# A graph layer and an attention layer on one core: late x one slot ahead, and a new order of vector work from the sixth values to the end of the projections

## The chip, the cores and the metric

The kernel runs on one core of one Trainium2 chip. The metric is the device time of one execution, in microseconds. A core has five engines that take their instructions in program order and wait for each other through semaphores: PE (TensorE, matrix products), DVE (VectorE), ACT (ScalarE), POOL (GpSimd) and SP (SyncE, which here only issues DMA transfers; ACT issues some too).

## The reference, cut to what matters

x has 64 batches of 256 nodes with 512 channels; adj is a 256 x 256 matrix of zeros and ones.

```python
# layer 0: graph
a = adj.astype(x.dtype); deg = a.sum(axis=1)
mi = einsum('bkd,od->bko', x, Wi);  mj = einsum('bkd,od->bko', x, Wj)
x = layernorm(x + deg[None, :, None] * (mi + b) + einsum('ij,bjo->bio', a, mj))
# layer 1: attention, 8 heads of 64 channels
q, k, v = (split_heads(x @ W.T + bias) for W, bias in (...))
attn = softmax(where(adj == 0, -inf, q @ k.T / 8))
x = layernorm(x + (attn @ v) @ Wo.T + bo)
```

All of it is float32.

## The kernel before

The 64 batches go in 32 groups of two. A batch is two tiles t = 1, 0 of 128 nodes. The steps of neighbouring groups are interleaved by hand: turn g of the loop at L1132 (31 turns) finishes the attention of group g, runs layer 0 for the batches b1 = 2(g+1) and b2 = b1 + 1 of the next group, and ends with the next group's projections to q, k and v and its first two scores. b3 = b1 + 2 is a batch whose x is fetched ahead.

Float32 products are split. A factor is cut into a head (rounded on ACT, `split_head`, L680), a diff (DVE, `split_diff`, L683: head times a constant minus the source) and a low part (source minus head, `split_low`, L686, on DVE or POOL as its argument says). A product is then three matrix products, into two PSUM banks: heads and lows into X, diffs into Y. ACT takes X out of its bank, DVE adds Y. The weights are kept in DRAM in this cut form and come through a ring of seven buffers (`factor`); `bring` (L445) fetches the next one when one has been used. In the loop its orders stand on SP, or on ACT in the middle of the output projection.

The attention of a group is eight pairs of heads w = 0 to 7, the first four for the first batch. For each, `scores` (L896) puts its products on PE at once and returns the rest as a function (`now()`, `later()`): DVE adds the mask (L910), ACT takes the exponential (L914), POOL adds two halves for the denominators (`pk`, L924). `values` (L935) is the product with v. `divide_two` (L954) runs after every second pair: ACT copies the values to aoT (L958), PE sums the denominators (`den`), DVE takes the reciprocal into `spread` (L1009), two DMAs copy halves of spread to the other partitions (L1012). `multiply` (L949) multiplies aoT by spread on POOL (L952). With `apart=True` the step from the reciprocal on is returned as `invert`; in the last one the sum of inverses is returned as `total_up`.

aoT is then cut for the output projection: `ao_parts(g, i, cs)` is batch i of the group, with the channel chunks `upper` (0, 1; pairs 0 and 1 of the batch) or `lower` (2, 3). The buffers of q, k and v are free by then and take the three parts, so that in the profile qT, kT and v hold head, diff and low part. `o_steps` (L821) is that projection: `begin` and `go_on` for the first batch's tile 0, `own` for its tile 1, `others` for the second batch's tiles, with `adds` for their sums on DVE (L830, L833). PE runs straight from `others` into the first values projection, `v[0]`, whose bank must have been freed by `adds(1)`.

Layer 0 of b1 and b2 are the objects `first` and `second`. `add` adds the neighbours' sum to x (DVE, L613), `stat` takes the statistics of layernorm (four DVE instructions, L496 to L502, and a power on POOL, L504), `give` applies them (two ACT instructions, L509, L510). The result h has to be turned for the projections: `send_h` writes a tile to DRAM (SP, L702), `fetch_h` reads it back in another order (SP, L707), `turn_h` turns it on DVE into hF (L517); then it is cut into hA, hD, hL. Within `others` the same is done for b2.

x comes twice: `load_x` (L294) for the sums, 512 KB into one of five buffers xh (the late x), and `load_xB` (L302), four DMAs, for the transposed form, which `turn_x` turns on DVE and `x_head`, `x_diff`, `x_low` cut on ACT, DVE and POOL. `finish_steps` (L875) gives six steps for the group that is done: `end[0]`, `end[2]` statistics, `end[1]`, `end[3]` their application, `end[4]`, `end[5]` the stores. `add_bias` and `add_output_bias` are two additions on POOL (L368, L733).

Every engine's order is that of the Python program: each instruction passes through

```python
    def in_order(ins):
        tc.keep_in_program_order(ins)
```

so the order of the calls in the loop is the order on each engine's queue, and two calls that use different engines can change places without changing either queue.

Of the kernel before, what the change touches and what calls it, by code (L numbers as in the profile page):

```python
# [219 lines left out]
def unshifted_path(ctx, tc, flag, x, adj, wiT, wjT, b0, wqT, bq, wkT, bk, wvT, bv, woT, bo, out):  # L220
# [16 lines left out]
    nc = tc.nc  # L237
# [56 lines left out]
    def load_x(b):  # L294
        if b < B:
            xh[b] = p5.tile([P, NT, D], F32, tag="xh", name="xh")
            in_order(nc.sync.dma_start(out=xh[b], in_=x[b].rearrange("(t p) d -> p t d", p=P)))
# [147 lines left out]
    def bring(several=1, left=1, issuer=None):  # L445
        for _ in range(several):
            if queue:
                name, j, first = queue.pop(0)
                f = stream.tile([P, 3, D], F32R, tag="factor", name="factor")
                coming.append(f)  # L450
                if first:
                    begin_make(f, name, j)
                    end_makes(left)
                else:
                    end_makes()
                    in_order((issuer or nc.sync).dma_start(out=f.bitcast(F32), in_=kept[name][j]))
# [216 lines left out]
    def three(tags):  # L673
        return [p1.tile([P, NC, NB * N], F32R, tag=t, name=t) for t in tags]
# [4 lines left out]
    def split_head(parts, src):  # L679
        in_order(nc.scalar.activation(parts[0], src, AF.Identity, scale=DOWN))  # L680
# [4 lines left out]
    def split_low(parts, src, engine):  # L685
        in_order(engine.tensor_tensor(parts[1], src, parts[0].bitcast(F32), ALU.subtract))  # L686
# [18 lines left out]
    def fetch_h(b, t):  # L705
        hB[b, t] = p1.tile([P, P // R, P], F32, tag=f"hB{t}", name="hB")
        in_order(nc.sync.dma_start(out=hB[b, t].rearrange("p a n -> p (a n)"),  # L707
                                   in_=h_cols[b][t].rearrange("q (r a) n -> (q r) (a n)", r=R)))
# [226 lines left out]
    def values(g, w):  # L935
        i, pr = divmod(w, NC)
        if w == 0:
            aoT[g] = p1.tile([P, NC, NB * N], F32, tag="aoT", name="aoT")
        pp = w % 2
        if pp == 0:  # L940
            pavs[g] = value_bank("pav").rearrange("p (r q) -> p r q", r=2)
        pe, _ = made[g, w]
        for kc in range(NT):
            for q in range(P // R):
                d0 = 2 * pr * DH + channels(q).start
                matmul(pavs[g][q * R:(q + 1) * R, pp ^ (q // 2), :], vv[g][:, i, kc, d0:d0 + R], pe[:, q % 2, kc, :],
                       start=(kc == 0), stop=(kc == NT - 1), tile_position=(0, q * R))

    def multiply():  # L949
        while products:  # L950
            d, spread = products.pop()
            in_order(nc.gpsimd.tensor_tensor(d, d, spread, ALU.mult))  # L952
# [34 lines left out]
    def ao_parts(g, i, cs):  # L987

        cols = slice(i * N, (i + 1) * N)
        return cut_parts(aoP[g], cs, cols), aoT[g][:, cs, cols]  # L990
# [32 lines left out]
    def run(steps):  # L1023
        for s in steps:
            s()
# [77 lines left out]
    v, q_, k = projection_steps(0, "SMSM", False)  # L1103
# [28 lines left out]
    for g in range(NG - 1):  # L1132
        b1, b2, b3 = NB * (g + 1), NB * (g + 1) + 1, NB * (g + 2)
        every, upper, lower = slice(0, NC), slice(0, 2), slice(2, NC)
        if g == 0:
            fold_value_bias()
            add_bias(b2)
            first.graph_half(1)
            first.take(1)
            first.cut_up(1)  # L1140
            make_first("wi", 0)
            first.graph_half(0)
            first.take(0)
            first.cut_up(0)
            make_first("wi", 1)
            first.own_half(0)
            end_makes()
        else:
            first.streamed = second.streamed = coming[1:1 + NC]
            k[NC - 1]()  # L1150
            x_head(b2)
            x_low(b2)
            add_bias(b2)
            first.graph_half(0, (0, 2, 1))
            first.take(0)
            x_diff(b2)
            first.own_half(1, kind="S")
            first.own_half(0, kind="S")
            first.cut_up(0)

        values(g, 0)
        values(g, 1)
        divide_two(g, 1)
        run([scores(g, 2), scores(g, 3)])
        load_xB(b3)
        second.own_half(1)
        if g == 0:
            make_first("wi", 2)
        second.own_half(0)
        if g:  # L1170
            for _ in range(NC):
                coming.pop(0)
                bring()

        values(g, 2)
        values(g, 3)
        multiply()
        if g == 0:
            make_first("wi", 3)
            end_makes()  # L1180
        early = cut_early(g)
        split_head(*early)
        divide_two(g, 3)
        now, later = scores(g, 4), scores(g, 5)
        now()
        second.graph_half(1, (0, 2, 1))
        second.take_x(1)
        later()
        second.take_y(1)
        split_diff(*early)  # L1190
        split_low(*early, nc.gpsimd)
        first.neighbours()
        second.graph_half(0, (0, 2, 1))
        second.cut_up(1)
        first.add(1)
        first.add(0)
        second.take(0)
        first.stat(1)
        second.cut_up(0)
        first.give(1)  # L1200
        send_h(b1, 1)

        values(g, 4)
        values(g, 5)
        load_x(b3)
        multiply()
        if g == 0:
            add_output_bias(0)
            add_output_bias(1)
        first.stat(0)  # L1210
        invert = divide_two(g, 5, True)
        now, later = scores(g, 6), scores(g, 7)
        aoP[g] = three(("qT", "kT"))
        aoP[g].insert(1, None)
        now()
        split_head(*ao_parts(g, 0, lower))
        begin, go_on, own, adds, others = o_steps(g, early[0], lambda t: turn_h(b2, t))
        begin()
        later()
        second.neighbours()  # L1220
        values(g, 6)
        invert()
        fetch_h(b1, 1)
        values(g, 7)
        split_diff(*ao_parts(g, 0, lower))
        second.add(0)
        aoP[g][1], = three(("v",))
        first.give(0)
        multiply()
        second.add(1)  # L1230
        send_h(b1, 0)
        total_up = divide_two(g, 7)
        split_head(*ao_parts(g, 1, upper))
        fetch_h(b1, 0)
        go_on()
        split_low(*ao_parts(g, 0, lower), nc.gpsimd)
        own()
        h11 = turn_h(b1, 1)
        split_head(*h11)
        second.stat(1)  # L1240
        second.give(1)
        split_low(*ao_parts(g, 1, upper), nc.vector)
        split_diff(*ao_parts(g, 1, upper))
        multiply()
        split_head(*ao_parts(g, 1, lower))
        second.stat(0)
        adds(0)
        split_low(*ao_parts(g, 1, lower), nc.gpsimd)
        second.give(0)
        split_diff(*ao_parts(g, 1, lower))  # L1250
        h10 = turn_h(b1, 0)
        send_h(b2, 1)
        send_h(b2, 0)
        split_diff(*h11)
        split_head(*h10)
        adds(1)
        split_low(*h10, nc.vector)
        split_diff(*h10)
        total_up()
        fetch_h(b2, 1)  # L1260
        fetch_h(b2, 0)
        split_low(*h11, nc.gpsimd)
        first, second = Layer0(b3) if b3 < B else None, Layer0(b3 + 1)
        v, q_, k = projection_steps(g + 1)
        end = finish_steps(g)
        others()
        turn_x(b3)
        if g == 0:
            make_first("wj", 0)
            make_first("wj", 1)  # L1270
        v[0]()
        if g == 0:
            make_first("wj", 2)
            make_first("wj", 3)
            end_makes()
        x_head(b3)
        x_low(b3)
        v[1]()
        x_diff(b3)
        load_xB(b3 + 1)  # L1280
        run([end[0], q_[0], end[1], k[0], end[2], q_[1]])
        if first:
            first.graph_half(1, (0, 2, 1))
            first.take(1)
        run([end[3], k[1], end[4]])
        add_output_bias(b1)
        if g + 2 < NG:
            add_bias(b3)
        run([q_[2]])
        load_x(b3 + 1)  # L1290
        add_output_bias(b2)
        if first:
            first.cut_up(1)
        run([k[2], q_[3], end[5]])
        turn_x(b3 + 1)
        run([scores(g + 1, 0), scores(g + 1, 1)])
        if g + 2 == NG:
            k[3]()
# [93 lines left out]
```

## Time and profile before

| what | value |
|---|---|
| median of 3 runs | 2952.39 us (2951.73 to 2953.07) |
| profiled execution: device time | 2951.97 us |
| profiled execution: span | 2950.1 us |
| PE busy | 2878.1 us (98%) |
| DVE, POOL, ACT busy | 2265.1, 1482.3, 1309.4 us |
| granted PE clock | 0.999 |
| one turn of the loop (from 1403.11 to 1493.52) | 90.41 us; PE 88.97, DVE 70.71, POOL 46.01, ACT 40.30 busy |
| HBM traffic | 227 GB/s over the span, 239 GB/s in that turn |

The profile is of one execution. A row of a timeline gives the start, the duration (of so many merged instructions, x1, x4), the engine, the source line, the operation, and out<-in by the program's names with shapes. A bracket at the end gives the time that the engine sat idle before it, and what ended that. Instructions of DVE, ACT and POOL overlap by about 0.1 us where one follows another at once. The ends of matmuls are modelled: the busy time of PE includes some slack that only shows in the distance between starts. PE's rows all have line L286, the helper through which it is issued.

### The profile page before, as it was taken

Reading aid. Unit: us, or ns where it says so; the run is one execution under the profiler, and the core shown is the slowest. Engines: PE = TensorE matmul, PEld = TensorE weight load, DVE = VectorE, ACT = ScalarE, POOL = GpSimd, SP = SyncE. Lnnn points to the kernel's source line nnn. Section 1 sums busy time; section 2 is a strip of 40 time slices with the busy share of each in tenths; the row PEclk is TensorE's granted clock in tenths of the full one; section 3 lists DMA queues with packets and bytes.
Section 4 is the critical chain, followed back from the end, with each engine's and each line's share of the span. In section 5 each row is a group of like instructions: output and inputs, shape, how many; then the busy total and the mean of one; then the engine's idle time right before and its main releaser. Section 6 shows DMA issues by size and latency. Waiting matters only on the chain.

```text
span 2950.1 us, 45509 instructions
## 1 busy us (share of the span) xinstructions
PE 2878.1 (98%) x16902; PEld 2140.1 (73%) x16902; DVE 2265.1 (77%) x3275; ACT 1309.4 (44%) x2412; POOL 1482.3 (50%) x1049
## 2 busy tenths in 40 slices
PE   9999999999999999999999999999999999999998
PEld 6577777777777777777777777777777777777775
DVE  5777787777877778877778777787777787777875
ACT  4444444444444444444444444444444444444443
POOL 3555555454555455454545544555545555454553
PEclk9999999999999999999999999999999999999999
DMA  7577766777666776667776677766677766777653
GB/s 251 194 258 239 247 218 218 255 245 266 217 219 239 266 247 230 212 226 264 242 247 222 221 249 252 268 212 215 238 267 240 246 214 215 257 248 261 213 211 116
DMA packets 303345, 690.54 MB, mean 234 GB/s; under 512 B 25744, under 2 KB 171280, under 8 KB 302864
## 3 DMA queue, kind: packets, MB, share of 16 engines
q1 hardware_dynamic: 282784, 588.02, 58.4%
q10 hardware_dynamic: 20336, 99.56, 9.5%
q8 instruction: 136, 2.23, 0.3%
q14 instruction: 89, 0.73, 0.1%
HBM read 589.04 MB, written 81.79 MB: 227 GB/s over the span
## 4 chain that ended last, share of the span: by engine, by line
PE 77%; DVE 15%; POOL 3%; DMA 3%; issue 1%; SPq 1%; ACT 1%; POOLq 0%; DVEq 0%; ACTq 0%
PE px L286 26%; PE pxy L286 20%; PE py L286 13%; PE ps L286 7%; PE pav L286 5%; PE pa L286 3%; DVE hF L517 2%; DMA hB<-h_cols 2%; DVE kT L683 2%; DVE spread L1009 2%; DVE st L496 2%; PE po L286 2%; DVE xh L833 1%; PE den L286 1%; DVE xh L830 1%
## 5 line engine op out<-in xcount | busy, mean ns | idle before, releaser
L924 POOL TENSOR_TENSOR pk<-pe 128x512 f32<-128x512 f32 x256 | 347.4, 1368 | 729.5 <-ACT pe L914 729.5
L914 ACT ACTIVATE pe<-pe 128x1024 f32<-128x1024 f32 x256 | 271.0, 1059 | 176.9 <-DVE pe L910 176.9
L504 POOL TENSOR_TENSOR rstd<-ve,mhalf 128x1 f32<-128x1 f32 x256 | 167.5, 654 | 343.4 <-DVE below L502 313.2
L910 DVE TENSOR_TENSOR pe<-ps,maskT 128x1024 f32<-128x1024 f32 x256 | 297.2, 1200 | 3.6 <-PE ps L286 3.6
L1009 DVE RECIPROCAL spread<-den 128x256 f32<-128x256 f32 x127 | 222.7, 1754 | 81.7 <-ACT aoT L958 51.8
L686 POOL TENSOR_TENSOR hL<-hF,hA 128x512 fp32r<-128x512 f32 x93 | 166.4, 1789 | 229.1 <-ACT hA L680 229.1
L774 DVE TENSOR_TENSOR kT<-py,kT 128x512 f32<-128x512 f32 x128 | 88.5, 692 | 226.2 <-ACT kT L773 226.2
L286 PE MATMUL ps<-qT,kT 64*128 64x256 f32 x2048 | 256.6, 390 | 0.0
L286 PE MATMUL pav<-pe,v_sb 128*32 128x256 f32 x4096 | 248.4, 382 | 3.5 <-DVE kT L774 1.5
L286 PEld LDWEIGHTS ps<-qT,kT 64*128 64x128 f32 x2048 | 187.3, 187 | 68.6 <-PE pav L286 26.3
L510 ACT ACTIVATE xh<-xh,shift,rstd 128x512 f32<-128x512 f32 x256 | 208.8, 816 | 8.6
L286 PEld LDWEIGHTS pav<-pe,v_sb 128*32 128x32 f32 x4096 | 120.0, 110 | 116.8 <-issue 24.4
L680 ACT ACTIVATE hA<-hF 128x512 fp32r<-128x512 f32 x124 | 78.3, 632 | 278.5 <-DVE hF L517 255.5
L286 PE MATMUL px<-factor,x_head 128*128 128x512 f32 x720 | 200.2, 400 | 0.0
L286 PE MATMUL py<-factor,x_diff 128*128 128x512 f32 x720 | 192.8, 390 | 2.0 <-ACT kT L773 2.0
L368 POOL TENSOR_TENSOR xh<-xh,degb 128x1024 f32<-128x1024 f32 x64 | 182.5, 2853 | 22.8 <-ACT degb L365 20.9
L286 PE MATMUL px<-factor,x_low 128*128 128x512 f32 x720 | 192.8, 390 | 0.0
L952 POOL TENSOR_TENSOR aoT<-aoT,spread 128x512 f32<-128x512 f32 x127 | 165.9, 1306 | 41.6 <-DMA spread<-spread 35.4
L686 POOL TENSOR_TENSOR x_low<-xT,x_head 128x1024 fp32r<-128x1024 f32 x60 | 144.2, 2403 | 67.6 <-ACT x_head L680 64.7
L286 PE MATMUL py<-hD,factor 128*128 128x512 f32 x640 | 175.9, 397 | 2.2 <-ACT kT L773 2.2
L286 PE MATMUL px<-hA,factor 128*128 128x512 f32 x640 | 175.7, 397 | 0.0
L496 DVE BATCH_NORM_STATS2 st<-xh 128x6 f32<-128x512 f32 x256 | 174.3, 681 | 0.2
(160 smaller groups left out, 6809.1 us busy)
## 6 DMA issues: line engine op xcount, KB each, us to landing
factor<-wi SPq DMA_DIRECT2D x120, 768.0 KB, 8.7
factor<-wo SPq DMA_DIRECT2D x120, 768.0 KB, 6.2
factor<-wv SPq DMA_DIRECT2D x93, 768.0 KB, 7.8
factor<-wk SPq DMA_DIRECT2D x93, 768.0 KB, 7.0
factor<-wq ACTq DMA_DIRECT2D x62, 768.0 KB, 7.6
factor<-wq SPq DMA_DIRECT2D x62, 768.0 KB, 7.4
xB<-in_x_dram SPq DMA_DIRECT2D x256, 128.0 KB, 4.1
xh<-in_x_dram SPq DMA_DIRECT2D x64, 512.0 KB, 3.9
```

What stands on the lines that cost most here:

```text
L286: in_order(nc.tensor.matmul(*args, **kw))
L368: in_order(nc.gpsimd.tensor_tensor(xh[b], xh[b], degb, ALU.add))
L496: order(nc.vector.bn_stats(st, t))
L504: order(nc.gpsimd.tensor_tensor(rstd, ve, mhalf, ALU.pow))
L510: order(nc.scalar.activation(t, t, AF.Identity, bias=shift, scale=rstd))
L686: in_order(engine.tensor_tensor(parts[1], src, parts[0].bitcast(F32), ALU.subtract))
L774: in_order(nc.vector.tensor_add(dst, Y, dst))
L910: in_order(nc.vector.tensor_add(pe.rearrange("p j t q -> p j (t q)"), ps.rearrange("p j t q -> p j (t q)"), maskT.rearrange("p t q -> p (t ...
L914: in_order(nc.scalar.activation(flat, flat, AF.Exp, scale=QSCALE, accum_out=etot[:, NB * g + i, pr:pr + 1]))
L924: in_order(nc.gpsimd.tensor_tensor(pk, pe[:, :, 0, :], pe[:, :, 1, :], ALU.add))
L952: in_order(nc.gpsimd.tensor_tensor(d, d, spread, ALU.mult))
L1009: in_order(nc.vector.reciprocal(rden, den))
```

## The change

`load_x(b3)` moves from after the sixth values (`values(g, 5)`) to before the third (`values(g, 2)`); it is behind the factors that `bring` fetches there. From the seventh scores to the end of the projections the calls are put in a new order. No call is added or left out. One changes its engine: the low part of b1's tile 0 (`split_low(*h10, ...)`) goes from DVE to POOL. The order on PE is the same as before.

On DVE: both `second.add` stand ahead of the first `split_diff`; `second.stat(0)` ahead of the upper `split_diff`; `x_diff(b3)` ahead of the sums of `v[1]`; `end[2]` after the sums of `q_[1]`; the `lo` of `first.cut_up(1)` after the sums of `k[2]`. On ACT: the split of the lower half of the first batch is ahead of the exponentials of `scores(g, 6)`; `end[3]` is after `k[1]`; `hi` of `cut_up` after `k[2]`. On POOL: `split_low(*h10)` after `split_low(*h11)`, and `add_bias(b3)` ahead of `add_output_bias(b1)`. On SP: `load_x(b3)` as said; the four DMAs of `load_xB(b3 + 1)` ahead of the four factors that `v[1]` brings; one factor ahead of `load_x(b3 + 1)`.

```diff
@@ 
                 bring()
+        load_x(b3)
 
         values(g, 2)
@@ 
         values(g, 5)
-        load_x(b3)
         multiply()
@@ 
+        split_head(*ao_parts(g, 0, lower))
         now()
-        split_head(*ao_parts(g, 0, lower))
         begin, go_on, own, adds, others = o_steps(g, early[0], lambda t: turn_h(b2, t))
         begin()
         later()
         second.neighbours()
         values(g, 6)
         invert()
+        second.add(1)
+        first.give(0)
+        values(g, 7)
+        aoP[g][1], = three(("v",))
         fetch_h(b1, 1)
-        values(g, 7)
+        second.add(0)
+        send_h(b1, 0)
+        multiply()
         split_diff(*ao_parts(g, 0, lower))
-        second.add(0)
-        aoP[g][1], = three(("v",))
-        first.give(0)
-        multiply()
-        second.add(1)
-        send_h(b1, 0)
         total_up = divide_two(g, 7)
-        split_head(*ao_parts(g, 1, upper))
-        fetch_h(b1, 0)
         go_on()
         split_low(*ao_parts(g, 0, lower), nc.gpsimd)
         own()
         h11 = turn_h(b1, 1)
+        second.stat(1)
+        split_head(*ao_parts(g, 1, upper))
         split_head(*h11)
-        second.stat(1)
         second.give(1)
+        multiply()
         split_low(*ao_parts(g, 1, upper), nc.vector)
-        split_diff(*ao_parts(g, 1, upper))
-        multiply()
+        fetch_h(b1, 0)
         split_head(*ao_parts(g, 1, lower))
         second.stat(0)
+        split_diff(*ao_parts(g, 1, upper))
+        split_low(*ao_parts(g, 1, lower), nc.gpsimd)
         adds(0)
-        split_low(*ao_parts(g, 1, lower), nc.gpsimd)
         second.give(0)
         split_diff(*ao_parts(g, 1, lower))
+        send_h(b2, 1)
         h10 = turn_h(b1, 0)
-        send_h(b2, 1)
-        send_h(b2, 0)
         split_diff(*h11)
         split_head(*h10)
+        total_up()
         adds(1)
-        split_low(*h10, nc.vector)
         split_diff(*h10)
-        total_up()
+        send_h(b2, 0)
         fetch_h(b2, 1)
-        fetch_h(b2, 0)
         split_low(*h11, nc.gpsimd)
+        split_low(*h10, nc.gpsimd)
...
+        fetch_h(b2, 0)
         others()
         turn_x(b3)
...
         v[0]()
+        load_xB(b3 + 1)
...
         x_head(b3)
+        x_diff(b3)
+        v[1]()
         x_low(b3)
-        v[1]()
-        x_diff(b3)
-        load_xB(b3 + 1)
-        run([end[0], q_[0], end[1], k[0], end[2], q_[1]])
+        end = finish_steps(g)
+        end[0]()
+        q_[0]()
+        end[1]()
+        k[0]()
+        q_[1]()
+        end[2]()
         if first:
             first.graph_half(1, (0, 2, 1))
             first.take(1)
-        run([end[3], k[1], end[4]])
-        add_output_bias(b1)
+        k[1]()
+        end[3]()
+        end[4]()
+        q_[2]()
         if g + 2 < NG:
             add_bias(b3)
-        run([q_[2]])
+        k[2]()
+        add_output_bias(b1)
         load_x(b3 + 1)
-        add_output_bias(b2)
         if first:
             first.cut_up(1)
-        run([k[2], q_[3], end[5]])
+        q_[3]()
+        end[5]()
         turn_x(b3 + 1)
+        add_output_bias(b2)
         run([scores(g + 1, 0), scores(g + 1, 1)])
```

More of the change, by code (lines that the diff above doesn't have):

```diff
@@ L1238, in unshifted_path @@
         h11 = turn_h(b1, 1)
+        second.stat(1)
+        split_head(*ao_parts(g, 1, upper))
         split_head(*h11)
-        second.stat(1)
         second.give(1)
+        multiply()
         split_low(*ao_parts(g, 1, upper), nc.vector)
-        split_diff(*ao_parts(g, 1, upper))
-        multiply()
+        fetch_h(b1, 0)
         split_head(*ao_parts(g, 1, lower))
         second.stat(0)
+        split_diff(*ao_parts(g, 1, upper))
+        split_low(*ao_parts(g, 1, lower), nc.gpsimd)
         adds(0)
-        split_low(*ao_parts(g, 1, lower), nc.gpsimd)
         second.give(0)
         split_diff(*ao_parts(g, 1, lower))
+        send_h(b2, 1)
         h10 = turn_h(b1, 0)
-        send_h(b2, 1)
-        send_h(b2, 0)
         split_diff(*h11)
         split_head(*h10)
+        total_up()
         adds(1)
-        split_low(*h10, nc.vector)
         split_diff(*h10)
-        total_up()
+        send_h(b2, 0)
         fetch_h(b2, 1)
-        fetch_h(b2, 0)
         split_low(*h11, nc.gpsimd)
+        split_low(*h10, nc.gpsimd)
         first, second = Layer0(b3) if b3 < B else None, Layer0(b3 + 1)
         v, q_, k = projection_steps(g + 1)
-        end = finish_steps(g)
+        fetch_h(b2, 0)
         others()
```

## The prediction

> **What bounds the kernel now.** I read the page first. TensorE is busy for nearly the whole span, at full clock; the chain of work that ended last lies 77% on PE.
>
> ```profile
> PE 2878.1 (98%) x16902; PEld 2140.1 (73%) x16902; DVE 2265.1 (77%) x3275; ACT 1309.4 (44%) x2412; POOL 1482.3 (50%) x1049
> ```
>
> The change leaves PE's instruction order alone, so only PE's waits can move. The list of waits, for PE alone:
>
> ```profile
> PE py L286 <- DVE kT L683: 20.6, 32, 0.7
> PE px L286 <- POOL v L686: 19.9, 31, 2.0
> PE pxy L286 <- DVE xh L833: 7.2, 30, 0.3
> ```
>
> Total, times, longest. Each comes about once in each of the loop's 31 turns; together they make 47.7 of the 62 us in the list. To see where, I took one ordinary turn in the timeline: it begins at 1403.11 (first px<-factor,early) and lasts 90.41 us. From 1411 to 1431 PE runs the output projection, then the first values products. PE there:
>
> ```profile
> 1411.76 0.73 PE L286 MATMUL px<-factor,v 128*128 128x512 f32 x2 [0.33 <-POOL v L686]
> ...
> 1417.98 0.50 PE L286 MATMUL py<-factor,kT 128*128 128x512 f32 x1 [0.72 <-DVE kT L683]
> ...
> 1421.01 0.50 PE L286 MATMUL pxy<-factor,hA 128*128 128x512 f32 x1 [0.23 <-DVE xh L833]
> ```
>
> Smaller slips hide under the 0.39 us of a modelled matmul whose real spacing is 0.227: py<-factor,kT starts 0.53 after its predecessor at 1414.24, py<-factor,hD 0.40 at 1422.21, px<-factor,hL 0.33 at 1430.15. A stalled matmul is also followed by a spacing of 0.34, so each stall costs 0.11 more. In this stretch DVE is busy 18.9 of 20 us: the stalls are DVE's queue. The same turn on DVE and POOL:
>
> ```profile
> 1412.90 0.68 DVE L686 TENSOR_TENSOR v<-aoT,qT 128x512 fp32r<-128x512 f32 x1
> 1413.50 0.68 DVE L683 SCALAR_TENSOR_TENSOR kT<-qT,aoT 128x512 fp32r<-128x512 f32 x1
> ...
> 1416.50 1.43 DVE L683 SCALAR_TENSOR_TENSOR kT<-qT,aoT 128x512 fp32r<-128x512 f32 x1
> ```
>
> ```profile
> 1409.16 1.30 POOL L952 TENSOR_TENSOR aoT<-aoT,spread 128x512 f32<-128x512 f32 x1 [1.02 <-DMA spread<-spread]
> 1410.42 1.29 POOL L686 TENSOR_TENSOR v<-aoT,qT 128x512 fp32r<-128x512 f32 x1
> 1413.01 0.98 POOL L504 TENSOR_TENSOR rstd<-ve,mhalf 128x1 f32<-128x1 f32 x1 [1.30 <-DMA spread<-spread]
> 1413.96 1.37 POOL L952 TENSOR_TENSOR aoT<-aoT,spread 128x512 f32<-128x512 f32 x1
> 1415.29 0.55 POOL L504 TENSOR_TENSOR rstd<-ve,mhalf 128x1 f32<-128x1 f32 x1
> 1416.08 1.30 POOL L686 TENSOR_TENSOR v<-aoT,qT 128x512 fp32r<-128x512 f32 x1 [0.23 <-ACT qT L680]
> 1417.33 1.75 POOL L686 TENSOR_TENSOR hL<-hF,hA 128x512 fp32r<-128x512 f32 x1
> ```
>
> The same kT instruction takes 0.68 at 1413.50 and 1.43 at 1416.50. The second began while POOL ran v (1416.08 to 1417.38) and ended at 1417.93, 0.55 after it; POOL's next, hL, is stretched in turn.
>
> **What the skill says.** SBUF — State Buffer, "Who interferes with whom": a DVE instruction with two SBUF inputs contends with a GpSimd instruction that reads SBUF, and whichever issued first holds the port for its whole length. The rows above agree: DVE loses 0.75. DVE's xh<-py (one input in PSUM) at 1415.89 ran 0.69 under the same POOL v, and neither was stretched. Perfetto Trace Analysis, "GPSIMD Engine Instruction": take such times by start-to-start spacing; I do. DMA: Bandwidth & Descriptors, "Issuing engines are not separate DMA queues": transfers of all queues interleave on the same 16 engines, so a 512 KB load can delay the small spread copies. Here those copies land 2.1 us after issue in the median, 7.6 at worst.
>
> **The change, part by part.** Names: in this stretch the buffers qT, kT and v hold the head, diff and low parts of aoT; "upper" and "lower" are aoT's halves for the turn's second batch (POOL's v at 1410.42 belongs to the first); h11, h10 are tiles 1 and 0 of h for the next group's first batch, h20 the last tile of its second. Times are in this turn, less 1400.
>
> *Late x.* Its 512 KB left SP at 3.46 and took 3.9 us to land, in front of the spread copies issued from 6.48. Now it leaves behind the three wv factors, some 15 us earlier; the other orders on SP up to there stay. The buffer is free by then: its old store leaves 52 us into a turn and lands 8.3 later, the load comes at 76. In this turn the copies were on time, so px<-v stays at 11.76; turns with waits up to 2.0 can gain, yet see below. It now stands before the previous pair's spread copies: issued at about 1391.5, landed by 1399.1 even at 7.6, plus 512 KB at the turn's 239 GB/s, 2.2, gives 1401.3, before POOL's aoT at 1401.80. Cost nothing, with 0.5 of cover at worst; past it, ACT's head split and exp 6 behind it would slip.
>
> *The ACT half split ahead of the exponential.* Exp 6 moves from 3.69 to about 3.91, exp 7 from 5.27 to 4.98; pav at 6.56 and den at 8.31 have their inputs. Nothing. *Both adds ahead of the first kT on DVE:* pa ends at 6.64, the adds take 1.28, kT 0.6: ready at 8.6, weights asked for at 9.0. Nothing, cover 0.4; beyond it PE waits one for one.
>
> *The DVE chain.* hF ran at 10.84, 0.17 after recip could let it go (10.67); with x out of the way hB should be there. From 10.67: stat(1), then v at 12.73. Stat(0), 1.07 long, now comes before the upper kT, which therefore issues at 14.40 instead of 13.50. That is where POOL meets it: POOL's rstd falls behind v on the port, and aoT begins 1.06 after v began, at 13.79, and holds the port 1.29, to 15.08 (its spread copies, issued at 10.79, land at 12.9). So kT ends 0.55 later, 15.63, and PE's py<-kT starts at 15.68 instead of 14.24. **This is a new wait**; behind it on DVE stand both adds, the lower kT, and h10's transpose.
> The adds (1.33 to the next start) bring the lower kT to issue at 16.88. POOL's rstd ends 0.41 after kT (16.04), its lower v runs to 17.31, so kT ends at 17.86. PE reaches it 2.86 after the upper one (14.24 to 16.87, and 0.23): 18.54. The 0.72 stall is gone, and its restart. PE's pxy<-hA follows 11 spacings later, 21.04. DVE: hF 17.78, hD issued 18.80, held by POOL's hL (to 19.01), ending 19.56; the adds that free the bank end at 20.88. No wait: 21.04 against 21.01.
> hL of h10 leaves DVE for POOL. DVE saves 0.60 (1420.87 to 1421.47); POOL runs it once ACT has the head, 19.6 to 20.9, in what was 4.85 us of idle time, and holds hD of h10 to 21.45. PE needs that at 21.95: the slip and restart are gone. px<-hL then starts at 22.18 instead of 22.55: 0.37 gained. DVE is 0.7 earlier from here, so h20's last hL comes before PE asks (it ended at 30.09 against PE's 30.15): slip and restart there, 0.10 each, are another 0.20.
>
> *Projections.* x_diff no longer waits for x_low (1.75 becomes about 1.1); x_low ends about 1.1 later, 35.8, wanted at 41.64. The v1 sums end 34.7; their bank is wanted at 38.01. The statistics, normalisations, stores and biases change places among gaps of DVE (2.67, 2.03, 1.02, 2.19) and POOL (9.61); no PE wait of 1432 to 1457 is on any of them. On SP the four xB loads (2.65) pass the wk and wq factors: the first leaves 2.4 later, 33.1, and lands by 40.1 at the median 7.0, wanted at 43.45. Nothing; if it were late, PE would wait at that product.
>
> **Sum.** 0.37 + 0.20 = 0.57 a turn, 31 turns: 17.7 us. 2950.1 becomes 2932.4 in the span, and the profiled execution (2951.97) lies within 0.5 of the median 2952.39, so the forecast is 2952.4 − 17.7 = 2935. Turns where px<-v was late by up to 1.5 gain more, since the new wait at kT swallows that. The order in which POOL and DVE take the port is not seen for these pairs: at best kT is not held at all, ready at 15.08, at worst it is held past POOL's next instructions; I take the middle, which is what every contested pair in this turn shows.
>
> **Rivals.**
> *Bigger gain.* The port costs nothing at the new places: upper kT 15.08, PE 15.14, bank free at 20.03, px<-hL at 21.64: 0.91 + 0.20 = 1.11 a turn, 34 us, 2918. Against it: the stretched rows.
> *The new wait takes all.* POOL's rstd gets the port before the waiting kT: 0.55 more, kT at PE 16.23, px<-hL 22.73; −0.18 + 0.20 = nothing, 2952. For it: aoT and rstd are back to back on POOL. Against: at 1417.38 DVE got in between v and hL.
> *Slower.* POOL keeps the port through the lower v as well (its head from ACT is ready at 15.73): v runs 15.75 to 17.05, kT ends 17.60, PE starts it at 17.65, 1.97 late; −1.97 + 0.57 = −1.40 a turn, 43 us, 2996. It decides from the point where PE starts the upper kT after 15.68 + 0.57 = 16.25. Against it: the same hand-over.
>
> **How the numbers follow.** Forecast 0.62, bigger 0.10, nothing 0.17, slower 0.11. A measurement here tells 0.2%, 5.9 us. The forecast's own range is 2924 to 2945 (0.25 to 0.9 a turn); it is faster save for 0.04. Faster: 0.58 + 0.10 + 0.05 of the third; same: 0.04 + 0.09; slower: 0.11 + 0.03. The range 2915 to 2951 leaves out the slower rival, half the third, and little else.
>
> **What would show it.** Right: in the waits, kT L683 stays on top, at about 30 x 1 us, on the upper kT; xh L833 nearly vanishes; DVE's upper kT has 1.2 us, ending 0.55 after POOL's aoT. Wrong: a PE wait on k1, x_low or the early kT; a third hold-up of kT; a period over 90.4.

## The result, and the profile after

| | before | after |
|---|---|---|
| median | 2954.20 us (2951.73 to 2958.41, 14 runs) | 2962.49 us (2957.10 to 2965.66, 14 runs) |
| ratio, 95% interval | | 1.0026 (1.0018 to 1.0034) |
| span of the profiled execution | 2950.1 us | 2961.9 us |
| granted PE clock | 0.999 | 0.995 |

The changed kernel is 0.26% slower; 2935 us, 0.6% faster, had been forecast. The page's line of busy times:

```profile
PE 2864.8 (97%) x16902; PEld 2147.2 (72%) x16902; DVE 2230.9 (75%) x3244; ACT 1308.2 (44%) x2412; POOL 1549.3 (52%) x1080
```

DVE has 31 instructions fewer and POOL 31 more: h10's low part. PE is busy for 13 us less in a span that is 12 us longer, so PE waits more. The list of waits, PE alone (total, times, longest):

```profile
PE py L286 <- DVE kT L683: 44.7, 28, 1.9
PE px L286 <- POOL v L686: 20.0, 31, 2.2
PE px L286 <- POOL hL L686: 8.6, 19, 0.7
```

kT went from 20.6 to 44.7 in total, the wait for xh L833 (7.2) is gone, the wait for POOL's v is as it was. A wait for POOL's hL is new, and no step of the prediction has it. One turn of after runs from 1863.94 to 1955.27, 91.33 long. PE's stalls in it, behind the short one at px<-v that before has too:

```profile
1876.59 0.50 PE L286 MATMUL py<-factor,kT 128*128 128x512 f32 x1 [1.63 <-DVE kT L683]
...
1890.80 0.50 PE L286 MATMUL py<-factor,hD 128*128 128x512 f32 x1 [0.23 <-DVE hD L683]
1891.95 0.50 PE L286 MATMUL px<-factor,hL 128*128 128x512 f32 x1 [0.65 <-POOL hL L686]
```

DVE and POOL in the same turn:

```profile
1875.33 1.20 DVE L683 SCALAR_TENSOR_TENSOR kT<-qT,aoT 128x512 fp32r<-128x512 f32 x1
...
1877.78 0.98 DVE L683 SCALAR_TENSOR_TENSOR kT<-qT,aoT 128x512 fp32r<-128x512 f32 x1
...
1888.24 1.11 DVE L517 STREAM_TRANSPOSE hF<-hB 128x512 f32<-128x512 f32 x1 [1.49 <-DMA hB<-h_cols]
```

```profile
1874.72 1.26 POOL L952 TENSOR_TENSOR aoT<-aoT,spread 128x512 f32<-128x512 f32 x1
1875.95 0.99 POOL L504 TENSOR_TENSOR rstd<-ve,mhalf 128x1 f32<-128x1 f32 x1
1876.91 1.29 POOL L686 TENSOR_TENSOR v<-aoT,qT 128x512 fp32r<-128x512 f32 x1
...
1890.09 1.80 POOL L686 TENSOR_TENSOR hL<-hF,hA 128x512 fp32r<-128x512 f32 x1 [4.12 <-ACT hA L680]
```

Read it backwards from the end. PE waits at 1891.95 for POOL's hL of h20, which follows ACT's head, which follows DVE's hF at 1888.24, and DVE had sat idle for 1.49 us until h20's fetch (hB) landed. DVE was no longer behind its own queue there: it waited for a DMA. Over the whole execution the profile of the buffer hB says how long DVE sat idle ahead of hF until a fetch landed (us in all, times), in before and then in after:

```profile
  DMA hB<-h_cols: 5.4, 11
```

```profile
  DMA hB<-h_cols: 29.1, 41
```

The fetch of h20 was issued at 1880.56 and took 7.6 us. ACT issued two factors (768 KB each) just ahead of it:

```profile
1879.98 0.32 ACTq L456 DMA_DIRECT2D factor<-wv  x1
...
1880.47 0.34 ACTq L456 DMA_DIRECT2D factor<-wq  x1
...
1880.56 0.33 SPq L707 DMA_DIRECT2D hB<-h_cols  x1
```

In the turn of before that the prediction is worked out in, the same fetch took 5.7, and it stood between the two factors:

```profile
1419.16 0.32 ACTq L456 DMA_DIRECT2D factor<-wv  x1
...
1419.41 0.33 SPq L707 DMA_DIRECT2D hB<-h_cols  x1
...
1419.60 0.37 ACTq L456 DMA_DIRECT2D factor<-wq  x1
```

Now it stands behind both. Averaged over 29 of the 31 turns (without the first and the last), in us after the start of the turn:

| | fetch of h20 issued | wq issued | fetch landed | hF of h20 |
|---|---|---|---|---|
| before | 16.48 | 16.61 | 21.78 | 23.44 |
| after | 16.82 | 16.76 | 23.61 | 23.74 |

The fetch leaves 0.34 later, because its normalisation waits for stat(0)'s power on POOL, which now stands behind aoT and the held-up kT (in the rows above it ends at 1876.94). It lands 1.8 later. That is one loss. The other shows only at PE. In some turns the matmuls after the kT wait run at half pace; here in the turn that begins at 1499.96:

```profile
1512.77 0.50 PE L286 MATMUL py<-factor,kT 128*128 128x512 f32 x1 [1.80 <-DVE kT L683]
...
1514.25 0.63 PE L286 MATMUL px<-factor,qT 128*128 128x512 f32 x1
1514.68 0.63 PE L286 MATMUL py<-factor,kT 128*128 128x512 f32 x1
...
1517.23 0.39 PE L286 MATMUL py<-factor,kT 128*128 128x512 f32 x1
1517.46 0.40 PE L286 MATMUL pxy<-factor,qT 128*128 128x512 f32 x1
```

The spacing from start to start is 0.43 from 1513.83 to 1517.23, 3.4 us, and 0.23 ahead of that and behind it. Here are two stretches of after (length, busy times, then the granted PE clock, DMA share, GB/s), the first in this turn, the second in the one at 1863.94:

```profile
1512.00:1518.00 6.00, 5.24 (x16) 4.13 (x17) 5.93 (x9) 2.87 (x7) 5.33 (x5) 0.72 0.57 144
...
1876.00:1882.00 6.00, 5.41 (x24) 4.39 (x25) 5.93 (x9) 2.77 (x6) 5.21 (x4) 1.00 0.60 148
```

Such a turn reaches px<-hL of h10 some 1.65 us later than an ordinary one. After has four of them among the turns whose px<-v was on time (a wait there of under 1.2 us), before has none.

### The profile page after: what moved, and what is told of

The parts are those of the page before. It is cut to its first block, busy times and chain, and to the rows that moved or that the text cites. A ratio compares the mean times of both kernels' runs of the same rounds, so it can differ in the third digit from the quotient of the medians.

```text
span 2961.9 us, 45480 instructions
## 1 busy us (share of the span) xinstructions
PE 2864.8 (97%) x16902; PEld 2147.2 (72%) x16902; DVE 2230.9 (75%) x3244; ACT 1308.2 (44%) x2412; POOL 1549.3 (52%) x1080
## 4 chain that ended last, share of the span: by engine, by line
PE 73%; DVE 14%; POOL 5%; issue 4%; DMA 3%; ACT 1%; SPq 1%; POOLq 0%; DVEq 0%; ACTq 0%
PE px L286 25%; PE pxy L286 17%; PE py L286 12%; PE ps L286 7%; PE pav L286 5%; PE pa L286 3%; DVE hF L517 2%; POOL hL L686 2%; DMA hB<-h_cols 2%; DVE spread L1009 2%; DVE st L496 2%; PE po L286 2%; DVE kT L683 2%; PE den L286 1%; DVE pe L910 1%
## 5 line engine op out<-in xcount | busy, mean ns | idle before, releaser
L924 POOL TENSOR_TENSOR pk<-pe 128x512 f32<-128x512 f32 x256 | 334.8, 1323 | 682.4 <-ACT pe L914 682.4
L504 POOL TENSOR_TENSOR rstd<-ve,mhalf 128x1 f32<-128x1 f32 x256 | 181.4, 709 | 361.1 <-DVE below L502 336.4
L686 POOL TENSOR_TENSOR hL<-hF,hA 128x512 fp32r<-128x512 f32 x124 | 206.0, 1661 | 197.5 <-ACT hA L680 195.0
L686 POOL TENSOR_TENSOR x_low<-xT,x_head 128x1024 fp32r<-128x1024 f32 x60 | 175.1, 2919 | 67.1 <-ACT x_head L680 64.1
```

What stands on the lines that cost most here:

```text
L504: order(nc.gpsimd.tensor_tensor(rstd, ve, mhalf, ALU.pow))
L924: in_order(nc.gpsimd.tensor_tensor(pk, pe[:, :, 0, :], pe[:, :, 1, :], ALU.add))
```

## The experiments

Times below are medians of 5 to 13 runs. Ratios are to the kernel before, timed beside each set (2954.59 for e1 to e4, 2953.78 for e5 to e8, 2953.55 for e9 to e12), with 95% intervals.

### Two parts that should cost nothing

e3_x_old_place is after with late x back:

```diff
-        load_x(b3)
 
         values(g, 2)
@@ 
         values(g, 5)
+        load_x(b3)
         multiply()
```

> The kernel after with one edit: the late x goes back to its old place after the sixth values. Theory (its place is of no weight: the spread copies and the first hB land within 0.1 us of where they landed before): within 2 us of the changed kernel, ratio to before 1.002 to 1.003. Rival (the early x crowds other transfers and makes the last hB late): 5 to 12 us faster than the changed kernel, ratio 0.9985 to 1.001.

e4_projections_old is after with everything behind `others()` in its old order, cut to its beginning:

```diff
         v[0]()
-        load_xB(b3 + 1)
...
         x_head(b3)
-        x_diff(b3)
-        v[1]()
         x_low(b3)
+        v[1]()
+        x_diff(b3)
+        load_xB(b3 + 1)
```

> The kernel after with the calls from the output projection's end to the end of the projections back in their old order. Theory (this part is hidden: no wait of PE there in either trace): within 2 us of the changed kernel, ratio to before 1.002 to 1.003. Rival (the xB loads ahead of the factors, or the statistics in another order, cost time): 4 to 12 us faster than the changed kernel, ratio 0.9985 to 1.001.

Measured: 2963.51 (ratio 1.0029, 1.0018 to 1.0041) and 2963.69 (1.0031, 1.0020 to 1.0042), both as slow as after. Late x's place and the projections' order, each put back alone, are worth nothing that can be measured; the loss lies between the sixth values and `others()`.

### The two losses, one at a time and together

e1_wq_behind_h20 is after with one factor's order moved on ACT, in `others`:

```diff
                 if c == 1:
-                    bring(issuer=nc.scalar)
                     h1 = turn(1)
                     split_head(*h1)
                     split_low(*h1, nc.gpsimd)
+                    bring(issuer=nc.scalar)
```

> The kernel after with one edit: in the output projection the order for the wq factor on ACT is given after the head split of the second batch's first tile, so that the last hB (h20's, 256 KB) has only the wv factor before it in the DMA rings. Theory (the last hB got behind a second 768 KB factor): hB lands at about 21.8 us of a turn instead of 23.6, PE's wait on POOL hL (8.6 us in all, 0.4 us a turn with its restart) nearly vanishes, 11 to 13 us less than the changed kernel: ratio to before 0.998 to 0.9995. The long wait on the upper kT and the turns at half clock stay. Rival (POOL, which now has one more hL, or DVE is what makes h20's hL late): hB lands earlier but the wait on hL stays, ratio 1.002 to 1.003.

e2_kT_before_stat is after with the upper kT back ahead of stat(0) on DVE:

```diff
-        second.stat(0)
         split_diff(*ao_parts(g, 1, upper))
+        second.stat(0)
         split_low(*ao_parts(g, 1, lower), nc.gpsimd)
```

> The kernel after with one edit: on DVE the upper kT goes back ahead of stat(0). Theory (the long wait on kT costs twice, by itself and by the half-clock stretches that follow it in some turns; and the later stat(0) made the last hB late): upper kT ready at about 11.2 us of a turn as before, POOL's aoT behind it, stat(0), give(0) and the last hB as early as before; lower kT held again to about 14.9; no turn at half clock beyond the one of before; what is left is hL of h10 on POOL: 0.3 to 0.5 us a turn better than before, 9 to 15 us, ratio to before 0.995 to 0.997. Rival (the loss sits elsewhere, in the projections or the late x): ratio to before 1.000 or more.

e5_both has both edits:

> The kernel after with both edits that helped it: the upper kT ahead of stat(0), and the wq factor issued behind the cuts of h20's predecessor. Theory (two separate losses, a new wait at kT and the h20 fetch caught behind two factors): the two gains add where they don't overlap; the kT wait and its slow stretches go (0.3 a turn), the wait at h20's hL goes (0.2 more than the edit at kT alone gives), so 2935 to 2939 us, 0.9935 to 0.995 of before, kT L683 at most 0.7 long, no POOL hL wait. Rival (PE only has 0.6 a turn to give in this stretch, and either edit takes it): 2941 to 2944, as each alone.

| | median | ratio | px<-hL of h10 | px<-hL of h20 | period |
|---|---|---|---|---|---|
| before | 2953.78 to 2954.59 | 1 | 19.59 | 27.21 | 90.57 |
| after | 2962.49 | 1.0026 | 19.63 | 27.65 | 90.98 |
| e1, wq later | 2941.35 | 0.9953 (0.9940 to 0.9967) | 19.47 | 27.07 | 90.30 |
| e2, kT ahead | 2943.77 | 0.9964 (0.9951 to 0.9976) | 19.28 | 27.01 | 90.29 |
| e5, both | 2936.90 | 0.9939 (0.9926 to 0.9953) | 19.30 | 26.90 | 90.13 |

(The last three columns are averages over the same 29 turns of the profiled execution: us after the turn's start, and from one start to the next.)

In e1 the kT wait is still there (45.5 us in all), and the wait for hL has left the list. The fetch lands at 21.83 on average, as expected, and DVE's idle time for hB is what it was before the change:

```profile
  DMA hB<-h_cols: 5.8, 13
```

A turn of it that begins at 1760.42: the fetch left at 1777.1, wq at 1780.08, and hF does not wait:

```profile
1783.14 1.11 DVE L517 STREAM_TRANSPOSE hF<-hB 128x512 f32<-128x512 f32 x1
```

This one order of one DMA is worth 21 us, where 11 to 13 had been expected. The expected part is there: from h10's px<-hL to h20's PE takes 7.60 instead of 8.02, 0.42 a turn or 13 us. The rest of the gain (0.16 ahead of it, of which two half-pace turns fewer make 0.11, and 0.10 behind it) was not expected, and its cause is open. In e2 the fetch leaves as early as in before (16.39), since stat(0)'s power no longer stands behind a held-up kT; DVE waits 11.4 us for hB in all, 21 times. The half-pace turns behind kT go too. The two gains overlap (21.1 and 18.7 us alone, 25.6 together), because stat(0) ahead of kT causes both losses. With both edits e5, inside its forecast, is the fastest of the kernels here, with e11 below, and beats before and after. Between e1 and e5 lie 4.4 us, but their intervals overlap: what the kT wait costs with the fetch in order is not settled better than that.

The half-pace turns sort themselves by the kT wait. Of 29 turns, those with a half-pace stretch here though px<-v was on time: after 4, e1 2, e3 3, e4 5; before, e2, e5 none. The granted clock in the traces also shows which waits do it. In every kernel with more than one stretch of half clock they begin on one grid with a step of 3.413 us: in after these four begin at 967.65, 1421.62, 1513.78 and 2240.82, which is 133, 27 and 213 steps apart. Now take PE's idle time within each step of that grid, in the loops of all kernels here but e8, whose waits are far longer. Of 227 steps with 1 to 1.75 us of it, none is followed by a step at half clock; of 23 with 1.75 to 1.85, 15 are; of 34 with more, 32 are. So it counts how a wait lies on the grid: of 60 single waits of 1.85 us or more, 23 are split so that no step holds 1.75 of them, and none of these is followed by half clock; of the other 37, 32 are. The waits at the upper kT, mostly 1.6 to 1.9 us, lie across that border; the 0.7 of before lies far below it. Waits at px<-v of 1.8 to 2.3 us do the same in most kernels, once in before and three times in after.

### What the gain is made of

e7_h10_low_on_pool is before with one edit of the change:

```diff
         adds(1)
-        split_low(*h10, nc.vector)
         split_diff(*h10)
@@ 
         split_low(*h11, nc.gpsimd)
+        split_low(*h10, nc.gpsimd)
```

> The kernel before with one edit of the change: the low part of h10 on POOL, behind that of h11. The prediction's price: the slip and restart at hL of h10 go (0.37 a turn) and DVE is 0.6 us earlier at h20 (up to 0.20 a turn): 11 to 18 us, 2935 to 2943, 0.994 to 0.996. Rival (PE meets the next late thing at once, or POOL's hL comes too late): 0.999 to 1.002.

e6_before_wq_behind_h20 is before with the diff of e1.

> The kernel before with the wq factor alone moved behind the cuts of h20's predecessor on ACT. Theory (in before the fetch still goes out 0.1 us ahead of wq, so nothing is caught): 0.997 to 1.000 of before, the landing of h20's fetch moves by under 0.5 us, and the slip at h20's hL (0.17 a turn, 5 us) goes at most. Rival (the factor's place is worth 20 us by itself, in any order of the vector work): 0.993.

Measured: e7 2939.63 (0.9953, 0.9939 to 0.9966), e6 2952.14 (0.9996, 0.9988 to 1.0004). The engine of one low part is the whole gain that can be told from zero: 14 us, the middle of the forecast for it. wq's place is worth nothing measurable where the fetch leaves ahead of it anyway, so e1's gain is the repair of what the new order broke. e5 is 2.7 us under e7, inside their intervals: the rest of the new order is worth at most a little.

### The caught fetch by itself

e8_stat0_behind_adds is before with stat(0) later and the upper kT where it was:

```diff
-        second.stat(0)
         adds(0)
+        second.stat(0)
```

> The kernel before with stat(0) moved behind the two adds of tile 0, the upper kT staying where it is: no new wait at kT, but h20's normalisation, its send and its fetch go out about 1.3 us later, behind the wq factor. Theory (the fetch is caught behind two factors): it lands 2.5 to 4 us later than in before, PE waits 1 to 2 us at h20's hL in each turn, 30 to 60 us slower (1.010 to 1.020), clock 0.999. Rival (the fetch shares the engines and lands only as much later as it goes out): 1.3 us later, a wait of at most 0.8, under 1.007.

Measured: 3131.78 (1.0604, 1.0589 to 1.0618), 178 us slower, 5.8 a turn. The direction is the theory's, the size three times its upper end. Here are DVE's idle time for hB, then PE's longest wait, then DVE in the turn that begins at 1773.59:

```profile
  DMA hB<-h_cols: 145.2, 44
```

```profile
PE pxy L286 <- DVE xh L833: 129.2, 31, 5.4
```

```profile
1796.50 1.13 DVE L517 STREAM_TRANSPOSE hF<-hB 128x512 f32<-128x512 f32 x1 [4.29 <-DMA hB<-h_cols]
```

I had counted one caught transfer, h20's fetch. Two others are caught, and that one isn't: it only leaves late. In that turn wv left at 1788.69, the send of h20 at 1789.1, wq at 1789.13, the fetch of h20's predecessor at 1789.62. The send took some 6.7 us (2.3 in before), so that h20's own fetch could leave at 1795.8 only (it then takes 2.7 on average), and the predecessor's fetch took 6.8 (2.7 in before), to 1796.4. DVE stands at the predecessor's hF, and behind it in its queue stand the adds that PE waits for. A delay of 1.3 us on DVE became 5.8 on PE. The clock fell to 0.978, which had not been expected either: behind waits of some 4 us come half-clock stretches. They make at most 69 of the 178 us, an estimate: 0.022 of the span of 3127.6.

### The contested port: the lower kT put between the adds

The lower kT's wait of 0.7 a turn looked like 20 us to be had. Four kernels put that kT between `add_x(0)` and `add_y(0)`, so that it is issued beside POOL's v instead of behind it:

```diff
-        adds(0)
+        one_add[0](0)
...
         split_diff(*ao_parts(g, 1, lower))
+        one_add[1](0)
```

`one_add` is the pair `(add_x, add_y)`, returned by `o_steps`.

e12_before_kT_between is before with this alone; e9_pool_h10_wq_kT_between adds the diffs of e7 and e1; e11_both_kT_between is e5 with it. e10_same_wv_wq_behind is e9 with the wv factor behind the same cuts as wq:

```diff
-                if c:
+                if c > 1:
                     bring(issuer=nc.scalar)
                 if c == 1:
                     h1 = turn(1)
                     split_head(*h1)
                     split_low(*h1, nc.gpsimd)
                     bring(issuer=nc.scalar)
+                    bring(issuer=nc.scalar)
```

> The kernel before with the lower kT between the two adds of tile 0, and nothing else. Port theory: the wait at the lower kT falls from 0.7 to under 0.3, and px<-hL comes 0.4 to 0.8 earlier in the turn; but PE, being earlier, frees the ring earlier, so the wq factor is issued ahead of h20's fetch and part is given back: 2925 to 2950. Rival (the crossing doesn't depend on PE's being earlier): 2922 to 2932. Rival (kT is as long at its new place): 2950.

> The kernel before with three edits: the low part of h10 on POOL, the wq factor issued behind the cuts of h20's predecessor, and the lower kT on DVE between the two adds of tile 0 instead of behind them. The price of the port as the prediction told it: kT then issues within 0.1 us of POOL's lower v, both let go by ACT's head; if it gets the port it is 0.68 long instead of 1.43 and DVE is 0.75 earlier from there; if POOL gets it kT ends with POOL's v, 0.5 earlier than now. Either way the wait at the lower kT (0.72 and a restart of 0.11) falls to under 0.3: 2915 to 2930, 0.987 to 0.992 of before. Rival (PE meets the add that was put back, at pxy, or the fetches caught behind the wv factor): no better than 2937.

> As the run before it, with the wv factor as well moved behind the cuts of h20's predecessor. Theory (with PE earlier the wv factor is issued ahead of the fetch of h20's predecessor and holds it up): 3 to 15 us faster than the run before it. Rival (that fetch isn't caught, and wv 3.7 us later comes late for its product): equal or slower, with a PE wait on DMA factor<-wv.

> The kernel after with upper kT ahead of stat(0), wq behind, and the lower kT between the adds of tile 0. If the rest of the new order is worth nothing, equal to the same edits on the kernel before (label e9) within 0.2%: 2915 to 2930. If it is worth something, faster by more than that.

| | median | ratio |
|---|---|---|
| e12 | 2962.88 | 1.0033 (1.0021 to 1.0045) |
| e9 | 2941.69 | 0.9960 (0.9946 to 0.9974) |
| e10 | 3000.46 | 1.0161 (1.0147 to 1.0174) |
| e11 | 2937.08 | 0.9946 (0.9933 to 0.9960) |

None does what the port theory says: e9 and e11 miss 2915 to 2930, and e12 is slower than each of its forecasts. DVE in e12, in the turn that begins at 1863.78:

```profile
1876.79 0.69 DVE L683 SCALAR_TENSOR_TENSOR kT<-qT,aoT 128x512 fp32r<-128x512 f32 x1 [0.18 <-ACT qT L680]
...
1879.00 1.45 DVE L683 SCALAR_TENSOR_TENSOR hD<-hA,hF 128x512 fp32r<-128x512 f32 x1
```

POOL there:

```profile
1876.84 1.81 POOL L686 TENSOR_TENSOR v<-aoT,qT 128x512 fp32r<-128x512 f32 x1 [0.23 <-ACT qT L680]
1878.61 1.30 POOL L686 TENSOR_TENSOR hL<-hF,hA 128x512 fp32r<-128x512 f32 x1
```

kT does get the port first and is 0.69 long instead of 1.43. But POOL's v is now held, 1.81 instead of 1.30, so POOL's hL starts later, over DVE's next instruction with both inputs in SBUF: hD is 1.45 long instead of 0.76. Of DVE's 0.75, 0.69 is handed back three instructions on, and PE's wait moves to the add behind it (28.5 us on xh L833 in place of 20.6 on kT). And since PE is earlier at the output projection, wv leaves at 15.63 on average instead of 16.17 and wq at 16.13 instead of 16.61, ahead of h20's fetch (16.56), which lands at 23.34 instead of 21.78. That fits e12's being slower than before; no kernel moves wq in e12 and nothing else, so it is not shown alone. With wq moved the place of kT is worth nothing: e9 is 2.1 us above e7, e11 0.2 above e5; and e9 and e11 agree within 0.2%, as e7 and e5 do. e10 did what its rival says, in PE's waits:

```profile
PE pxy L286 <- DMA factor<-wv: 52.1, 31, 2.6
```

wv has no slack of 4 us; wq, 3.7 us later in e6, has it. With both factors behind it, h20's fetch in e10 lands 2.7 us after it leaves.

## Why the prediction was wrong

*Late x* was priced at nothing, and e3 and an unmoved px<-v (8.98 after the turn's start in both) say so. But its aside, that with x out of the way h11's hB would let hF start 0.17 earlier, failed: hF starts at 7.83 on average, before 7.85.

*ACT's half split and the adds ahead of the first kT*: no wait appeared there. Right.

*The new wait at the upper kT* was right in mechanism, and so was the hold-up in size: kT is 1.20 long behind POOL's aoT (forecast 1.2), PE at 12.74 in the median turn (15.68 less the start at 3.11 is 12.57). The "about 30 x 1 us" for PE's wait doesn't fit these figures: PE's last matmul ahead of it ends at 14.10 (1413.71, 0.39 long), so from there to 15.68 the wait is 1.58, and 28 x 1.6 was measured. That length matters below. The Trainium skill's SBUF — State Buffer, "Who interferes with whom", on which this rests, agrees with the contested pairs shown here. That the lower kT's wait and the one at pxy<-hA go was right too. e12 adds what the step did not ask: such a lock is paid by somebody, and one has to follow whom.

*hL of h10 gains 0.37.* In the median turn it gained 0.19 (19.45 to 19.26); the missing 0.18 is about what hF did not start earlier. On average it lost 0.04, because of the four half-pace turns: 4 × 1.65 / 29 = 0.23. No step had them; the clock was put at nothing without a reason. The Trainium skill has the effect, TensorE: Matmul & The Clock Gate, "Part 1: The HAM clock gate (the "warmup" mystery)": half rate after an idle window of some 3.4 us, and the windows run freely. The length and the fixed grid agree. But here some 1.8 us of idle time within one window was enough, which the waits at kT reached in about one turn of seven.

*"DVE is 0.7 earlier from here, so h20's last hL comes before PE asks"*, 0.20 gained. **This is the step that failed**: PE lost 0.40 there on average (27.65 − 27.21 = 0.44, less the 0.04 above). It took DVE's queue for what sets h20's hF, gave no time to h20's fetch, and looked at orders on SP alone. The factors on ACT's queue belong to the same race. In before the fetch left 0.13 us ahead of wq on average. In after stat(0)'s power, held up on POOL, made it leave 0.34 later, 0.06 behind wq, and now its landing sets hF (23.61 and 23.74). The Trainium skill's DMA: Bandwidth & Descriptors, "Issuing engines are not separate DMA queues", which I had cited, says that the queues interleave; they do here, but the order of issue across the two queues counted to 0.1 us. In after, e3 and e4 the 13 fetches that left over 0.05 ahead of wq took 5.4 on average, and the 72 that left over 0.05 behind it 6.9. It is not all that counts: in e2 27 of 29 left ahead of wq and took 6.0.

*Projections* were priced at nothing, and e4 says so.

The sum then: 0.04 + 0.40 lost and 0.03 won back behind it, 0.41 a turn; 31 turns make 12.7, against 11.8 us in the spans and 8.3 in the medians. The rivals all lay in the contested port. The one that said "slower" wanted a third hold-up of kT, and that did not happen.

## What to carry to other kernels

When a step that sends something through a DMA moves, list the large transfers of every queue near its issue, not of its own alone, and how many tenths lie between; here a fetch that slipped behind one more factor lost 1.5 us. When a wait on a shared port is taken from one instruction, ask which instruction of the other engine now ends later, and what that one runs into. A forecast of a new wait of PE that comes near 1.8 us should carry a term for its clock.

## What the runs showed of the hardware that I had not expected

- How long a 256 KB transfer takes to land depends on the 768 KB ones that left within about 1 us ahead of it, on either issuing engine: h20's fetch took 2.7 us with none ahead (e10), 4.8 to 5.3 with wv ahead (before, e1, e5, e6, e9, e11) and 6.8 with wv and wq ahead (after, e12), as averages of 29 turns. It is no strict order: e2 and e7, where wq left some 0.1 us behind the fetch as in before, took 6.1 and 5.7, and in e8 the send, 0.4 us behind wv and 0.1 ahead of wq, took 6.7 instead of 2.3. The exact rule is open.
- A PE idle time of some 1.8 us can start a 3.4 us stretch at half clock, if it falls within one step of a grid of 3.413 us. At the upper kT it did in 14 of the 96 turns of after, e1, e3 and e4 in which px<-v was on time, each time with a wait of 1.76 to 1.87 us, and there in no such turn of before, e2, e5 and e7. In e10 three of the waits for wv, of 1.9 to 2.6 us, did it.
